# Attention over paged keys on one core: the read of the turned probabilities, one set of tables and one score change their places

## The chip, the cores and the metric

The kernel runs on one core of a Trainium2 chip. The metric is the device time of one execution in microseconds (us), as the median of several executions. The same kernel was also executed once under the hardware profiler; the views of the profile come from that one execution.

The core's engines each work through their own list of instructions, in order: PE (TensorE, the matrix multiplications, with PEld for the loads of its weights), DVE (VectorE), ACT (ScalarE), POOL (GpSimd) and SP (SyncE). An engine waits where its next instruction needs something that another engine or a transfer hasn't delivered, and all that stands behind it on the same engine waits too. Transfers between the core's memory and DRAM are issued by SP, ACT and POOL, each of which has a queue of its own, and are carried out by 16 DMA engines that all queues share.

## The reference

The input x has 8 sequences of 128 rows and 512 columns. Two layers follow, all in f32:

```python
x = x + L0_ffn(L0_cond(x, ...))        # weights picked by sequence; experts of rank 16
x = x + L1_ffn(L1_cond(x, ...))        # attention over a paged cache; 64 small experts
```

The change lies in the attention, L1_cond, which takes most of the time:

```python
q = x @ Wq.T ; k = x @ Wk.T ; v = x @ Wv.T      # 32 query heads, 8 key heads, 128 wide
q, k = rope(rmsnorm(q), pos), rope(rmsnorm(k), pos)
kc = k_cache[block_table] ; vc = v_cache[block_table]   # 16 pages of 32 keys for each sequence
scores = q @ [kc, k].T * SCALE                  # 512 cached keys and 128 new ones
scores = where(valid, scores, -1e30)
o = softmax(scores) @ [vc, v]
y = o @ Wo.T                                    # 4096 -> 512, summed over all heads
```

Four query heads share one key head.

## The kernel before

**Units and turns.** The attention is cut into 64 units. A unit is one sequence and one key head with its four query heads; two units that follow each other have the same sequence and the same half of the key heads, and share one set of gathered pages. Such a pair is called a step. The units are worked through in turns, and turn u holds work of several units at once: the scores and the softmax of unit u, the weighted sum of the values of unit u-2 (`values`), the output product of unit u-3 (`output`, `add_output`), and the projection and the norms of units that come later. The order on every engine is the one in which the code calls these helpers. That order is what the change edits.

**The products by fewer multiplications.** The projection and the output product work on pairs of sequences with 7 products in place of 8, so sums of inputs and weights are made beside them: `sums_x` and `sums_q` (their sum is recorded at line L163) for the projection, `sums_o` (L1031) for the output. Depending on u mod 4 and u mod 16 a turn holds different such work. The kinds u mod 4 = 0, 1, 2, 3 last differently for this reason; in turns with u mod 16 = 13, two of the sums of the projection's weights are done on DVE.

**A turn, in the order of the code** (`iteration`):

1. The pages of the *next* step. Turn u with u even gathers the first 8 of its 16 key pages, turn u odd the last 8: SP reads a page's number and issues a transfer of 32 KB (`gather`, L193) for each. Five are issued, then `exchange_in(u - 1)`, then the other three. So the keys of a step are complete when the last three pages of an odd turn have landed, and the first score of the following even turn needs them.
2. `exchange_in(u - 1)`: two reads on SP of what unit u-1 has written to DRAM, the turned queries and keys of unit u+1 (`qkb`, L933, 320 KB) and the turned probabilities of unit u-1 (`pT`, L936, 1280 KB, into one of two buffers that alternate).
3. `gather_v` (L203, POOL): two of the step's four groups of value pages, by an indirect transfer.
4. `make_tables` (L236, POOL): two products that hold the tables of the rotation for a step. It is called in turns 3, 5, 7, ... for the step of unit u+3; turn 3 makes those of step 3.
5. For each of the four query heads h: `scores(u, h)` on PE (L439: 128 x 512 against the pages; L442: 128 x 128 against the new keys), `mask_exp` (DVE L452 adds the mask and finds the lowest value, ACT L463 takes the exponential with its sum), `normalize` of the head before (DVE L468 the reciprocal, POOL L469 the product), at h = 2 `blocks_qk` (DVE L425: queries and keys of unit u+2, turned by blocks of 32 x 32, into the buffer `pb`), at h = 2 and 3 `blocks` (DVE L474: the probabilities turned by blocks, into `pb`), then `output(u - 3, h)` on PE (L1081) and, for h > 0, a product of the projection (PE L262, its sums on DVE L265).
6. `add_output(u - 3, ...)` (DVE L1150 and L1168: the sums of the output into `yp`), in an early and a late part; `heads_qk(u + 1)` (ACT L943: `qkb` into the order of the heads), `norms(u + 3)` (ACT L311 and L313, POOL L315 and L317).
7. The rest of `blocks`, then `exchange_out(u)` (L486): `pb` is written to DRAM as `px` in four transfers of 400 KB, two issued by SP and two by ACT.
8. `rotate(u + 3)` (DVE L329 to L347) and last on PE `values(u - 2)` (L956: ten passes of 512 columns that read `pT`).

**Who has how many buffers.** `pb` has one: `blocks_qk` of turn u writes it first, and so must wait until `px` of turn u-1 has been read out of it completely. `pT` has two, `px` in DRAM three. The banks into which PE writes scores are two, so a score needs the bank that `mask_exp` of the score before the last has read; the output product has one bank, `y`, and so its first product in a turn must wait for the `add_output` of the turn before.

**The full turn into DRAM and back.** What runs through one round: `blocks_qk` and `blocks` fill `pb`, `px` goes out, in the next turn `qkb` and `pT` come in; `qkb` is wanted at that turn's end by `heads_qk`, `pT` by `values` at the end of the turn after it. SP's queue holds, in this order and for each turn: five pages, `qkb`, `pT`, three pages, and SP's half of `px`.

Of the kernel before, what the change touches and what calls it, by code (L numbers as in the profile page):

```python
# [30 lines left out]
GH = 2  # L31
# [27 lines left out]
def adaln_ffn_kernel(  # L59
# [122 lines left out]
    def gather(step, first=0, end=NPP):  # L182
        hf, b = divmod(step, B)
        if first == 0:
            kv_t[step] = (
                kvp.tile([P, NPP, GH, PSIZE], F32, tag="kt", name=f"kt_{step}"),
                kvp.tile([P, LC, GH * D], F32, tag="vt", name=f"vt_{step}", bufs=3),
            )
        kt, vt = kv_t[step]
        for j in range(first, end):  # L190
            at = b * NPP + j
            page = nc.sync.value_load(pg[0:1, at : at + 1])
            nc.sync.dma_start(  # L193
                out=kt[:, j, :, :].rearrange("p g t -> p (g t)"),
                in_=kc[hf, ds(page, 1)].rearrange("o p f -> p (o f)"),
            )
# [237 lines left out]
    def scores(u, h, which=None):  # L434
        st, g = units[u]
        kt, _ = kv_t[st]
        qkT = qkT_t[u]
        s = banks(f"s_{u}_{h}", which)
        nc.tensor.matmul(  # L439
            out=s[:, :L], lhsT=qkT[:, h, :], rhs=kt[:, :, g % GH, :], start=True, stop=True  # L440
        )
        nc.tensor.matmul(  # L442
            out=s[:, L:NK], lhsT=qkT[:, h, :], rhs=qkT[:, REP, :], start=True, stop=True
        )
        s_t[u, h] = s

    def mask_exp(u, h):

        st, g = units[u]
        p = pp.tile([P, NK], F32, tag="p", name=f"p_{u}_{h}")  # L450
        low = stat.tile([P, 1], F32, tag="low", name=f"low_{u}_{h}")
        nc.vector.tensor_tensor_reduce(  # L452
            out=p,
            in0=s_t.pop((u, h))[:, :NK],
            in1=mask_t[st],
            scale=rs_t[u][:, h : h + 1],
            scalar=BIG,
            op0=ALU.add,
            op1=ALU.min,
            accum_out=low,  # L460
        )
        den = stat.tile([P, 1], F32, tag="den", name=f"den_{u}_{h}")
        nc.scalar.activation(p, p, AF.Exp, bias=low, scale=-1.0, accum_out=den)  # L463
        p_t[u, h], den_t[u, h] = p, den
# [460 lines left out]
    with ExitStack() as l1:  # L925
# [1 line left out]
        wk2 = l1.enter_context(tc.tile_pool(name="l1_2", bufs=2))  # L927

        def exchange_in(u):
            m = px_t.pop(u).rearrange("k b i f -> (k b) i f")  # L930
            if u + 2 in range(4, NU):
                qkb = wk1.tile([P, QD, NH * 32], F32, tag="qkb", name=f"qkb_{u + 2}")
                nc.sync.dma_start(out=qkb, in_=m[:, :, PW:])  # L933
                qkb_t[u + 2] = qkb
            pT = wk1.tile([P, QD, PW], F32, tag=f"pT{u % 2}", name=f"pT_{u}")
            nc.sync.dma_start(out=pT, in_=m[:, :, :PW])  # L936
            pT_t[u] = pT
# [325 lines left out]
        def iteration(u):  # L1263

            on = lambda v: 0 <= v < NU
            fb = LAST.get(u)
            r, group = u % 16, (u // 16 + 1) * GH
            f = room(fb) if fb is not None else None

            if u % 4 == 3:  # L1270
                k, j, four = (u + 5) // 4, 0, True
            elif u % 4 == 0:
                k, j, four = (u + 4) // 4, 0, False
            elif u % 4 == 1:
                k, j, four = (u + 3) // 4, 1, True
            else:
                k, j, four = (u + 2) // 4, 1, False
            slots = ()
            if 2 < u and k < NU // 4:
                slots = (1, 2, 6) if four else (4, 5, 3)  # L1280
            st = u // GH
            pages = on(u) and 1 < st + 1 < NQ * B
            first, end = ((0, 8), (8, NPP))[u % GH]
            if pages:
                gather(st + 1, first, first + 5)
            if on(u - 1):
                exchange_in(u - 1)
            if pages:
                gather(st + 1, first + 5, end)
            if pages:  # L1290
                gather_v(st + 1, u % GH * LC // GH, (u % GH + 1) * LC // GH)
            if on(u + 3) and u % GH == 1 and u > 1:
                make_tables(units[u + 3][0])
            if on(u - 3) and u % 4 == 3 and (u - 3) // 4 < WHOLE_PAIRS:
                load_y((u - 3) // 4)
            if u == 1:
                load_o(0, (0, B11), (2, B21))
            if NU - 5 <= u < NU - 1:
                load_whole(NQ * B - 4 + u - NU + 5)
            z_exchange(u - NU + 3)  # L1300
            if on(u - 3):
                evict_o(u - 3)
            if u >= NU and fb is not None:
                yT_t[fb] = f_turn(fb, *f)
            if u > NU:
                z = u - NU - 1
                z_turn(z, lambda n, shape: wo_t[:, slot(T4, NQ - 1), z * DM : (z + 1) * DM].rearrange("p (c s) -> p c s", c=NC))
            if u >= NU:
                z_blocks(u - NU + 4)
            if u in (2, 3):  # L1310
                norms(u + 3)
            for h in range(REP):
                if on(u):
                    if (u, h) not in ((1, 0), (1, 1), (2, 0)):
                        scores(u, h)
                        mask_exp(u, h)
                    if h > 0 and (u, h) != (1, 1):
                        normalize(u, h - 1)

                    if (u, h) == (1, 2):  # L1320
                        transpose_qk(3)

                    sums_o(u, h)
                    sums_w(u, h)
                    if 16 <= u < NU - 8 and (r, h) == (2, 3):
                        load_o(u // 16, (1, B12))

                    if h == 2:
                        new_pb(u)
                        if u + 2 in range(4, NU):  # L1330
                            blocks_qk(u + 2, u)
                    if h > 1:
                        blocks(u, h - 2)
                    if h == 1 and u == NU - 5:
                        f_fold()
                    if h == 3:
                        z_blocks(u - NU + 4)
                    if h == (1 if u == NU - 3 else 2) and fb is not None:
                        yT_t[fb] = f_turn(fb, *f)
                if on(u - 3):  # L1340
                    output(u - 3, h)
                    sums_a(u - 3, h)
                if h > 0 and slots:
                    project(k, j, slots[h - 1 : h])

                if (u, h) in WHOLE:
                    project_whole(1, *WHOLE[u, h])
            if on(u - 3):
                add_output(u - 3, False)
            if on(u + 1) and (u + 1) % GH == 0:  # L1350
                make_mask(units[u + 1][0])
            if u + 1 in range(4, NU):
                heads_qk(u + 1)

            if u < NU - 8:
                if r in LOADS_Q and u < NU - 16:
                    for n, i in LOADS_Q[r]:
                        load_q(group + n, i)
            if NU - 8 < u < NU - 2:
                f_weights(u - NU + 7)  # L1360
            if on(u):
                normalize(u, REP - 1)
            if 3 < u < NU - 3:
                norms(u + 3)
            if u == 1:
                scores(2, 0)
                mask_exp(2, 0)
            if on(u):
                blocks(u, REP - 2)
                blocks(u, REP - 1)  # L1370
                exchange_out(u)
            if on(u - 3):
                add_output(u - 3, True)
            if 16 <= u < NU - 8 and r in (0, 1, 2):
                n = u // 16
                load_o(n, *{0: ((0, B11),), 1: ((2, B21),), 2: ((3, slot(B22, n)),)}[r])
            if u == NU - 6:
                load_o(NQ - 1, (1, B12))
            if u + 3 < NU:
                rotate(u + 3)  # L1380
                if four and slots:
                    project(k, j, (7,))

            if u == NU - 6:
                rooms()

            ahead = u >= NU
            if ahead and on(u - 2):
                values(u - 2)
            if fb is not None:  # L1390
                f_gate(fb, *f_project(fb, yT_t.pop(fb), *f), *f)
            if not ahead and on(u - 2):
                values(u - 2)
# [164 lines left out]
```

## Time and profile before

| | before |
|---|---|
| runs | 1205.39, 1205.78, 1211.27 us |
| median of the runs | 1205.78 us |
| the profiled execution, its own time | 1209.55 us |
| span of its trace | 1207.8 us |
| mean granted clock of TensorE | 1.0 |
| DMA, mean over the span | 250 GB/s, 302.31 MB |
| SP's and ACT's queues, share of 16 engines | 53.2% in the one, 13.6% in the other |

The first layer ends at about 125 us; the turns take most of what follows. The lines below are the page's strip of 40 equal slices of the span, with each engine's busy share in tenths:

```profile
PE   9999999999999999999999999999999999999998
DVE  2647788787888787878887887879887888787632
POOL 3545769778755686578647685687657784643100
PEclk9999999999999999999999999999999999999999
DMA  8823777888888988888789978887989888898742
```

A digit 9 stands for 90% or more. PE is at 9 in every slice but the last, DVE and the DMA engines at 7 to 9 through the turns. The granted clock is full throughout.

The most costly groups on the other engines (line, engine, operation, out and in, count; then busy us, mean ns of one, idle us just before, and what ended most of it):

```profile
L463 ACT ACTIVATE p<-p,low 128x640 f32<-128x640 f32 x256 | 211.8, 828 | 433.7 <-DVE den L468 267.4
L469 POOL TENSOR_SCALAR p<-p,den 128x640 f32<-128x640 f32 x256 | 210.2, 822 | 233.4 <-DVE den L468 232.5
L452 DVE CUSTOM_DVE_ANT_0 p<-s,mask,rs 128x640 f32<-128x640 f32 x256 | 222.3, 878 | 81.6 <-PE s L442 80.7
L474 DVE STREAM_TRANSPOSE pb<-p 128x640 f32<-128x640 f32 x248 | 204.8, 826 | 25.6 <-POOL p L469 25.5
L203 POOL DMA_INDIRECT vt<-in_vc,vrow x128 | 137.6, 1075 | 40.8 <-issue 31.9
```

Idle time of ACT and POOL costs nothing by itself; it says only what they wait for.

### The profile page before, as it was taken

What the parts mean: (1) busy time and instruction counts of PE and PEld (TensorE: products, weight loads), DVE (VectorE), ACT (ScalarE), POOL (GpSimd) and SP (SyncE); (2) the same over time, 40 slices, a digit from 0 to 9 for tenths busy, and PEclk for the clock granted to TensorE, in tenths of its full rate; (3) what the DMA queues carried; (4) which work ended last, traced back from release to release, by engine and by line L of the source; (5) the groups of instructions that cost most, each with busy time, mean ns of one, the idle gap of its engine ahead of it and who ended that gap; (6) DMA issues with size and microseconds to landing.
All of it is one profiled execution on the core that took longest, in us unless ns stands there. A gap on an engine that the chain in (4) does not pass through costs nothing.

```text
span 1207.8 us, 16783 instructions
## 1 busy us (share of the span) xinstructions
PE 1194.7 (99%) x4156; PEld 714.6 (59%) x4156; DVE 913.1 (76%) x2103; ACT 504.3 (42%) x1457; POOL 740.4 (61%) x828
## 2 busy tenths in 40 slices
PE   9999999999999999999999999999999999999998
PEld 7666545565555556555556555555656555555554
DVE  2647788787888787878887887879887888787632
ACT  1345534443444444444444444444444444443211
POOL 3545769778755686578647685687657784643100
PEclk9999999999999999999999999999999999999999
DMA  8823777888888988888789978887989888898742
GB/s 315 287 89 113 247 238 245 263 265 264 264 253 257 301 244 278 260 287 282 237 258 282 294 240 281 285 289 246 279 255 302 254 263 251 261 281 230 232 140 97
DMA packets 205300, 302.31 MB, mean 250 GB/s; under 512 B 84755, under 2 KB 119316, under 8 KB 204180
## 3 DMA queue, kind: packets, MB, share of 16 engines
q1 hardware_dynamic: 170308, 196.81, 53.2%
q10 hardware_dynamic: 18576, 52.04, 13.6%
q0 software_dynamic: 16320, 52.40, 12.4%
q8 instruction: 33, 0.54, 0.2%
q14 instruction: 63, 0.52, 0.1%
HBM read 185.44 MB, written 115.74 MB: 249 GB/s over the span
## 4 chain that ended last, share of the span: by engine, by line
PE 82%; DMA 6%; POOL 4%; DVE 3%; issue 2%; SPq 1%; ACT 1%; ACTq 0%; DVEq 0%; POOLq 0%
PE o L956 18%; PE p L262 18%; PE s L439 16%; PE y L1081 13%; PE s L442 4%; PE p L295 3%; DMA px<-pb 2%; PE op L1445 2%; PE y L1094 2%; PE bp L648 1%; PE cp L626 1%; DMA kt<-in_kc 1%; PE fr L866 1%; POOL p L469 1%; DVE pb L474 1%
## 5 line engine op out<-in xcount | busy, mean ns | idle before, releaser
L463 ACT ACTIVATE p<-p,low 128x640 f32<-128x640 f32 x256 | 211.8, 828 | 433.7 <-DVE den L468 267.4
L469 POOL TENSOR_SCALAR p<-p,den 128x640 f32<-128x640 f32 x256 | 210.2, 822 | 233.4 <-DVE den L468 232.5
L452 DVE CUSTOM_DVE_ANT_0 p<-s,mask,rs 128x640 f32<-128x640 f32 x256 | 222.3, 878 | 81.6 <-PE s L442 80.7
L262 PE MATMUL p<-wqkv,xo 128*128 128x384 f32 x784 | 281.1, 487 | 0.7 <-DVE c L265 0.3
L439 PE MATMUL s<-kt,qkT 128*128 128x512 f32 x504 | 258.7, 595 | 4.5 <-DMA kt<-in_kc 2.6
L956 PE MATMUL o<-pT,vt 128*128 128x512 f32 x512 | 230.2, 592 | 0.0
L474 DVE STREAM_TRANSPOSE pb<-p 128x640 f32<-128x640 f32 x248 | 204.8, 826 | 25.6 <-POOL p L469 25.5
L1081 PE MATMUL y<-wo,oT 128*128 128x256 f32 x784 | 206.6, 380 | 0.9 <-DVE yp L1168 0.5
L262 PEld LDWEIGHTS p<-wqkv,xo 128*128 128x128 f32 x784 | 148.2, 190 | 70.2 <-POOL wqkv L163 1.6
L442 PEld LDWEIGHTS s<-qkT 128*128 128x128 f32 x504 | 95.8, 190 | 120.5 <-issue 120.5
L203 POOL DMA_INDIRECT vt<-in_vc,vrow x128 | 137.6, 1075 | 40.8 <-issue 31.9
L956 PEld LDWEIGHTS o<-pT,vt 128*128 128x128 f32 x512 | 97.2, 190 | 107.8 <-issue 92.8
L439 PEld LDWEIGHTS s<-kt,qkT 128*128 128x128 f32 x504 | 94.2, 190 | 78.3 <-issue 32.5
L1081 PEld LDWEIGHTS y<-wo,oT 128*128 128x128 f32 x784 | 131.9, 191 | 9.8 <-PE s L442 1.2
L311 ACT ACTIVATE sq<-c 128x128 f32<-128x128 f32 x320 | 98.8, 309 | 9.5 <-DVE oT L474 1.4
L442 PE MATMUL s<-qkT 128*128 128x128 f32 x504 | 96.8, 274 | 0.0
L317 POOL TENSOR_TENSOR rs<-ss,mhalf 128x5 f32<-128x5 f32 x64 | 82.2, 1284 | 5.3
L979 ACT COPY oT<-o 128x512 f32<-128x512 f32 x64 | 37.4, 585 | 102.3 <-PE o L956 77.2
L315 POOL TENSOR_SCALAR ss<-ss,eps 128x5 f32<-128x5 f32 x64 | 27.6, 431 | 74.3 <-ACT sq L311 74.3
L956 PE MATMUL o<-pT,vn 128*128 128x512 f32 x128 | 65.4, 592 | 0.0
L425 DVE STREAM_TRANSPOSE pb<-ca 128x640 f32<-128x640 f32 x60 | 50.2, 836 | 18.1 <-DMA px<-pb 8.2
L265 DVE TENSOR_TENSOR c<-c,p 128x384 f32<-128x384 f32 x84 | 44.9, 534 | 22.9 <-PE p L262 22.7
(198 smaller groups left out, 1441.3 us busy)
## 6 DMA issues: line engine op xcount, KB each, us to landing
pT<-px SPq DMA_DIRECT2D x64, 1280.0 KB, 6.6
px<-pb SPq DMA_DIRECT2D x120, 400.0 KB, 5.2
px<-pb ACTq DMA_DIRECT2D x120, 400.0 KB, 4.2
qkb<-px SPq DMA_DIRECT2D x60, 320.0 KB, 3.4
kt<-in_kc SPq DMA_DIRECT2D x512, 32.0 KB, 5.1
wqkv<-in_wqkv POOLq DMA_DIRECT2D x32, 384.0 KB, 4.8
wo<-in_wo POOLq DMA_DIRECT2D x17, 512.0 KB, 7.5
yd<-yp POOLq DMA_DIRECT2D x12, 512.0 KB, 9.0
```

The costliest lines, as they stand in the source:

```text
L203: nc.gpsimd.indirect_dma_start(out=kv_t[step][1][:, c, :], out_offset=None, in_=vc, in_offset=bass.IndirectOffsetOnAxis(ap=vrow[:, hf, at ...
L262: nc.tensor.matmul(out=ps, lhsT=xo[:, pr, x, c, :], rhs=w[:, c, :], start=(c == 0), stop=(c == 1))
L311: nc.scalar.activation(sq, cs[:, at : at + D], AF.Square, accum_out=ss[:, h : h + 1])
L317: nc.gpsimd.tensor_tensor(rs, ss, mhalf, ALU.pow)
L439: nc.tensor.matmul(out=s[:, :L], lhsT=qkT[:, h, :], rhs=kt[:, :, g % GH, :], start=True, stop=True)
L442: nc.tensor.matmul(out=s[:, L:NK], lhsT=qkT[:, h, :], rhs=qkT[:, REP, :], start=True, stop=True)
L452: nc.vector.tensor_tensor_reduce(out=p, in0=s_t.pop((u, h))[:, :NK], in1=mask_t[st], scale=rs_t[u][:, h : h + 1], scalar=BIG, op0=ALU.add, ...
L463: nc.scalar.activation(p, p, AF.Exp, bias=low, scale=-1.0, accum_out=den)
L469: nc.gpsimd.tensor_scalar(p_t[u, h], p_t[u, h], den, 1.0, ALU.mult, ALU.mult)
L474: nc.vector.transpose(pb_t[u][:, :, h * w : (h + 1) * w].rearrange("p i (j a) -> p j i a", a=32), p_t.pop((u, h)).rearrange("p (j i a) -> ...
L956: nc.tensor.matmul(out=o, lhsT=vt[:, c, j * D : (j + 1) * D] if c < LC else vn_t.pop(u), rhs=pT[:, c], start=(c == 0), stop=(c == LC),)
L1081: nc.tensor.matmul(out=y_t["y"][:, half * HN : (half + 1) * HN], lhsT=part(key)[:, i * S : (i + 1) * S], rhs=wo_t[:, slot(w, key[0] // (B ...
```

## The change

Three edits, each of which moves instructions and adds or removes none.

1. `exchange_in(u - 1)` keeps the read of `qkb` only. The read of `pT` becomes `probs_in(u - 1)`, called after the turn's last three pages. On SP's queue the order becomes five pages, `qkb`, three pages, `pT`, SP's half of `px`.
2. `make_tables(3)`, on POOL, is called in turn 2 behind the last `normalize`, no longer in turn 3 behind `gather_v`.
3. In the turns 5, 9, 13, ..., 61 the second score and its `mask_exp` are called ahead of the first head's output product, not behind it. On PE the order becomes score 0, score 1, output product 0, and then as before. DVE, ACT and POOL have the same order as before, since nothing of theirs stands between the two calls.

```diff
         def exchange_in(u):
-            m = px_t.pop(u).rearrange("k b i f -> (k b) i f")
+            m = px_t[u].rearrange("k b i f -> (k b) i f")
             if u + 2 in range(4, NU):
                 qkb = wk1.tile([P, QD, NH * 32], F32, tag="qkb", name=f"qkb_{u + 2}")
                 nc.sync.dma_start(out=qkb, in_=m[:, :, PW:])
                 qkb_t[u + 2] = qkb
+
+        def probs_in(u):
+            m = px_t.pop(u).rearrange("k b i f -> (k b) i f")
             pT = wk1.tile([P, QD, PW], F32, tag=f"pT{u % 2}", name=f"pT_{u}")
             nc.sync.dma_start(out=pT, in_=m[:, :, :PW])
             pT_t[u] = pT
...
                 exchange_in(u - 1)
             if pages:
                 gather(st + 1, first + 5, end)
+            if on(u - 1):
+                probs_in(u - 1)
             if pages:
                 gather_v(st + 1, u % GH * LC // GH, (u % GH + 1) * LC // GH)
-            if on(u + 3) and u % GH == 1 and u > 1:
+            if on(u + 3) and u % GH == 1 and u > 3:
                 make_tables(units[u + 3][0])
...
             for h in range(REP):
                 if on(u):
-                    if (u, h) not in ((1, 0), (1, 1), (2, 0)):
-                        scores(u, h)
-                        mask_exp(u, h)
+                    ahead = u > 1 and u % 4 == 1
+                    for n in (((0, 1), (), (2,), (3,)) if ahead else ((0,), (1,), (2,), (3,)))[h]:
+                        if (u, n) not in ((1, 0), (1, 1), (2, 0)):
+                            scores(u, n)
+                            mask_exp(u, n)
                     if h > 0 and (u, h) != (1, 1):
                         normalize(u, h - 1)
...
             if on(u):
                 normalize(u, REP - 1)
+            if u == 2:
+                make_tables(3)
             if 3 < u < NU - 3:
                 norms(u + 3)
```

`GH` is 2 (units in a step), `REP` is 4 (query heads of a unit), `NU` is 64.

## Prediction

> **What bounds the kernel now.** I read the page's busy shares first, then the costliest groups, the waits of TensorE, the timeline around them, and last the DMA issues.
>
> ```profile
> PE 1194.7 (99%) x4156; PEld 714.6 (59%) x4156; DVE 913.1 (76%) x2103; ACT 504.3 (42%) x1457; POOL 740.4 (61%) x828
> L439 PE MATMUL s<-kt,qkT 128*128 128x512 f32 x504 | 258.7, 595 | 4.5 <-DMA kt<-in_kc 2.6
> L1081 PE MATMUL y<-wo,oT 128*128 128x256 f32 x784 | 206.6, 380 | 0.9 <-DVE yp L1168 0.5
> L425 DVE STREAM_TRANSPOSE pb<-ca 128x640 f32<-128x640 f32 x60 | 50.2, 836 | 18.1 <-DMA px<-pb 8.2
> ```
>
> TensorE is busy all the time, so a change that removes no matmul can win only the small idle times; the third number behind the bar is all the idle ahead of the scores (4.5 us) and of the output products (0.9 us). The last line is the one place where VectorE stands waiting for a write of the turned probabilities (px).
>
> ```profile
> PE s L439 <- DMA kt<-in_kc: 2.6, 2, 1.6
> PE s L439 <- ACT oT L979: 0.7, 1, 0.7
> PE s L439 <- PE o L956: 0.6, 2, 0.4
> PE y L1081 <- DVE yp L1168: 0.5, 1, 0.5
> PE y L1081 <- DVE yp L1150: 0.4, 1, 0.4
> DVE pb L425 <- DMA px<-pb: 8.2, 11, 1.3
> ```
>
> The shown idle is too small. Eight passes of 512 columns last 3.60 us at 0.59 each, so they start (3.60-0.59)/7 = 0.43 apart, and a modelled end lies 0.16 behind the next possible start. I therefore count a stall from start to start:
>
> ```profile
> 567.94 0.38 PE L442 MATMUL s<-qkT 128*128 128x128 f32 x2
> 568.74 1.10 PE L1081 MATMUL y<-wo,oT 128*128 128x256 f32 x4 [0.41 <-DVE yp L1150]
> 577.27 0.54 SPq L933 DMA_DIRECT2D qkb<-px  x1
> 577.86 0.62 SPq L936 DMA_DIRECT2D pT<-px  x1
> 579.01 2.02 SPq L193 DMA_DIRECT2D kt<-in_kc  x3
> 584.26 1.02 PE L956 MATMUL o<-pT,vn 128*128 128x512 f32 x2
> 584.89 0.81 SPq L486 DMA_DIRECT2D px<-pb  x2
> 586.33 1.10 PE L439 MATMUL s<-kt,qkT 128*128 128x512 f32 x2 [1.04 <-DMA kt<-in_kc]
> 577.29 0.84 DVE L425 STREAM_TRANSPOSE pb<-ca 128x640 f32<-128x640 f32 x1 [0.69 <-DMA px<-pb]
> ```
>
> Turn 30's first score could start at 584.26 + 2 x 0.43 = 585.12 and starts at 586.33: 1.21 us lost. Its keys are the three pages issued from 579.01 on, behind the 1280 KB of pT. Done for every first score on new keys (even turns), the stalls are 1.76 (turn 4), 0.38 (14), 0.83 (18), 0.17 (24), 1.21 (30), 0.12 (34), 0.14 (52) and 0.59 (58): 5.2 us; in each the last page's packets end 0.7 to 1.25 us before the score starts, also where the waits view names ACT or PE. The pass behind each is some 0.08 late: 0.6. The output products of turns 13 and 29 lose 0.63 and 0.58 (568.74 against 567.94 + 0.22) and 0.15 on the passes behind them: 1.4. Sum: 7.2 us that the change can reach. All stalls of TensorE together are 17.9 us; 5.9 of these lie ahead of attention and the rest elsewhere.
>
> **The probabilities read behind the last three pages.** No instruction is added. The pages are issued 1.15 us sooner (at 577.86 instead of 579.01), and the transfer that stood ahead of them goes behind them.
>
> ```profile
> pT<-px SPq DMA_DIRECT2D x64, 1280.0 KB, 6.6
> px<-pb SPq DMA_DIRECT2D x120, 400.0 KB, 5.2
> px<-pb ACTq DMA_DIRECT2D x120, 400.0 KB, 4.2
> qkb<-px SPq DMA_DIRECT2D x60, 320.0 KB, 3.4
> kt<-in_kc SPq DMA_DIRECT2D x512, 32.0 KB, 5.1
> ```
>
> The gain of a page is bounded below by the sooner issue, 1.15, above by this plus the 3.55 us that pT's packets take of all 16 engines: 4.7. The lower end clears every stall but 0.06 in turn 30 and 0.6 in turn 4, the middle clears all; I take all, 5.8 with the passes behind, the low end being 5.1.
>
> Price: three page issues took 2.6 us from first to the one that would follow (10.83, 11.71 and 12.59 us after px's issue on the mean of turns 4 to 55), so pT is issued about 2.6 us later. Who waits for pT is values, a turn and more later; that is hidden, with some 10 us of cover. What stands behind pT on SP's queue is px of the same turn (584.89), which waits for VectorE anyway, so the issue isn't delayed. But pT's packets now end later than px's issue: before, the last one ends on the mean exactly at px's issue (from 3.0 before to 2.8 after). With 2.6 us more and the engines' share in those bins (0.55 to 0.8 busy today), 0.85 to 1.0 us of all engines' work is left when px is issued, against 0.09 today.
>
> What that does to px, the trace bounds from two sides. Turns 14 and 46 had 1.05 us of pT left, and px landed 9.24 and 8.93 us after its issue against 8.07 on the mean: 0.8 to 1.1 us later for each us left. Over all turns, though, px's landing grows only 0.08 us for each us that pT ends later. So px lands 0.1 to 1.0 later; I take 0.8, from the two turns that look like the changed ones.
>
> The Trainium skill (DMA: Bandwidth & Descriptors, section on queues, rings and completion order) has a rule that speaks against the edit: a DMA engine takes the descriptors of one issuer's ring in order and takes turns between rings by packet. By that SP's half of px stands behind all that is left of pT, and only ACT's half takes turns. Turns 14 and 46 agree with it, the slope over all turns doesn't; by the rule every turn's px would be later by all that is left, by the slope by nearly nothing.
>
> Who waits for px: the transpose of queries and keys (L425), which writes the single buffer pb that px is read from. It starts at the earliest 0.44 after px's last packet, and px's next issue comes 6.64 after it (mean; at least 6.4). The ring is 8.07 + 0.44 + 6.64 = 15.15 against an undisturbed mean turn of 16.15 (14.21, 17.23, 15.94, 17.23 for the four kinds): 1.0 us free. Queued behind the waiting L425 on VectorE are the transposes of the probabilities, the sums of the projection and mask_exp of the next score, for which TensorE's banks wait. In 18 turns L425 waits 0.5 us or more already; stalls of TensorE followed in 3, 13 and 29 alone. I therefore price 0.8 in an ordinary turn at nothing, covered by the 1.0, and at the full delay of about 1.0 where VectorE has no gap: turn 3, where px(2) and the pages collide today, and turns 13, 29 and 45, which have the 2.55 and 0.94 us of weight sums (L163) on VectorE. 4 turns x 1.0 = 4.0; bounds 0 (the slope) and +22 (the rival below). If the cover of 1.0 is gone, every turn pays what lies beyond it.
>
> **Turn 3's tables made in turn 2.** GpSimd's 0.83 + 0.97 us at 146.67 move ahead of turn 3's value pages (1.09 + 1.33). In turn 3 the sums of squares behind them (L315, 148.44) had their last input from ACT at 148.23, so at most 0.2 is won; the value pages come 1.8 later and are read some 50 us on. Bounds: 0.3 either way; taken as 0.
>
> **Second score ahead of the output in turns 5, 9, ..., 61.** On TensorE two passes of 0.43 and two of 0.11, 1.08 us, go ahead of the first output product, which therefore has 1.08 more for its wait on yp: this covers 0.63 and 0.58. The other engines keep their order. The output then comes 1.08 later, and its consumer add_output stands at the turn's end. Gain 0 to 1.4; taken as 1.4, since the products' wait is all there is. If VectorE is late beyond 1.08, the third score's bank waits instead.
>
> Sum: -5.8 - 1.4 + 0 + 4.0 = -3.2 us. On the profiled execution's own 1209.55 us (span 1207.8 and 1.75 around it) this is 1206.3; that execution is 3.8 above the median of the runs, 1205.78, and on the median it is 1202.6.
>
> **Rivals.**
> *Full gain.* The late px costs nothing, as the slope says, and 7.2 go: 1198.6. For it: no stall in 15 of the 18 turns in which L425 waits today. Against it: turns 14 and 46, and shares of the DMA engines near 1.0 in the six us after px's issue, where a delay isn't made good.
>
> *The px ring takes over (slower).* Place: L425's wait for px in every turn; it decides once px lands more than 1.0 later on the mean. A later px makes the reads of the next turn later, so pT's rest grows with the delay. At a ring of 15.15 + delay, pT would end 12.3 + 6.6 - 15.15 = 3.7 us past px's issue rather than 2.6; the added 1.1 at a share of 0.8 makes 1.85 us left, times 0.8 a delay of 1.4 to 1.5, so 0.4 a turn more than the free 1.0. Over 56 turns +22, less 7: 1221. With 0.3 a turn, 1215. For it: L425 is the only wait of VectorE for px, and 18 turns are at its edge. Against it: a mean of 0.85 left is below the point.
>
> *It does nothing that shows.* The first score waits for something else at the same moment (rotated queries through ACT, or the banks), and the stall stays: 1205.8. Against it: qkb lands 1.35 us or more ahead of its use, and the pages' packets end last at all eight stalls.
>
> **How the numbers follow.** Forecast 0.45, its own range 1199.8 to 1206.5 (costs between 1.2 and 8); full gain 0.27; the ring 0.20; nothing 0.08. A measurement of this kernel tells 0.5%, 6.0 us, from no change. Faster than 1199.75 are most of the full gain (0.23) and the edge of the forecast (0.04): 0.27. Slower than 1211.8 is the ring without its mild end (0.17) and a forecast with turns 3, 13, 29 and 45 mis-sized (0.02): 0.19. The rest, 0.54, is within. The range runs from just below the full gain, 1197.5, to a mild ring, 1213; half of the ring's chance lies above it.
>
> **What would show it.** Right: no idle ahead of L439 from kt, pages' packets ending 2 us or more before each even turn; pT's packets ending 2 to 3 us past px's issue; px landing near 8.9; L425's wait grown from 8.2 us to 20 or more without a longer undisturbed turn; no idle ahead of L1081 from yp. Wrong: turns 36 to 39 longer than 14.21, 17.23, 15.94 and 17.23 (the ring), px landing at 8.1 (full gain), or first scores that still start late with their pages long there.

## The result, and the profile after

The changed kernel takes 1219.24 us in the median of 6 runs (1217.17 to 1223.87), the kernel before, run beside it, 1206.33. The ratio is 1.0108, with a 95% interval from 1.008 to 1.0137: 13 us slower, where 3 us less had been forecast.

The profiled execution took 1223.87 us, with a span of 1222.0. Of its 14.2 us over the span before, 2.9 are there by the end of turn 2: in the first 20 us the granted clock of TensorE was 0.83 in this execution and 1.0 in the one before, and at 38 us, ahead of anything that the change touches, TensorE is already 2.9 us behind. The other 11.3 us come in turns 3 to 60.

The costliest groups of the changed kernel's page (line, engine, operation, out and in, count; busy us, mean ns, idle us ahead and what ended most of it):

```profile
L262 PE MATMUL p<-wqkv,xo 128*128 128x384 f32 x784 | 282.3, 488 | 8.1 <-POOL wqkv L163 4.4
L425 DVE STREAM_TRANSPOSE pb<-ca 128x640 f32<-128x640 f32 x60 | 50.4, 840 | 62.3 <-DMA px<-pb 45.0
```

L425 stood idle for 18.1 us before and for 62.3 now; the projection's idle time grew from 0.7 to 8.1. TensorE's waits in the changed kernel (us in total, times, longest):

```profile
PE p L262 <- POOL wqkv L163: 4.4, 6, 1.2
PE p L262 <- DVE c L265: 3.8, 4, 2.7
PE s L439 <- DVE low L452: 3.8, 4, 1.6
...
PE y L1084 <- DVE yp L1153: 1.9, 2, 1.4
```

No wait for key pages is left: that part of the change did what it says. In its place stand waits for DVE and for GpSimd's weight sums, none of which was longer than 0.5 us before. GpSimd itself stands idle ahead of none of these sums (L163): it comes to them late, though the loads of the weights land later as well (6.7 us after their issue, 4.8 before). On the chain of work that ended last, which the page follows back from the last instruction, px's transfers have 11% of the span; before they had 2%. Last the page's DMA issues, with the median us to landing:

```profile
px<-pb SPq DMA_DIRECT2D x120, 400.0 KB, 6.3
px<-pb ACTq DMA_DIRECT2D x120, 400.0 KB, 8.0
...
kt<-in_kc SPq DMA_DIRECT2D x512, 32.0 KB, 3.0
```

A page lands 3.0 us after its issue instead of 5.1. The medians of px's writes, 5.2 and 4.2 before, can't be compared with these: of ACT's 120 writes the trace before tells the landing of 2 alone, the trace after that of 62. So I go by the packets. In turns 4 to 59, pT's rest at px's issue is 1.75 us of all engines' time (0.09 before), SP's half of px ends 7.48 us after its issue (6.52), ACT's half, the one that counts, 8.63 (8.05).

**Turn by turn.** I measured each turn from one end of `values` to the next and took its excess over the shortest that the same turn has in any profiled execution of this study. Before, the excess is 6.8 us in even turns, where new keys are first used, and 3.6 in odd ones; after, 2.9 and 18.8. The even turns 4, 14, 18, 24, 30, 34 and 58 won 5.6 us. Most other turns are the same to 0.01 us. The loss sits in few: against before, turn 3 is 1.9 us longer, 5 0.9, 9 0.6, 11 0.5, 13 1.3, 25 0.5, 27 0.7, 29 2.3, 37 0.4, 41 2.8, 43 2.3, 45 0.8, 52 0.5 and 60 1.4.

Turn 41 shows how. SP's issues, then DVE and TensorE, from the timelines of the changed kernel:

```profile
765.86 2.02 SPq L193 DMA_DIRECT2D kt<-in_kc  x3
767.97 0.61 SPq L939 DMA_DIRECT2D pT<-px  x1
772.37 0.81 SPq L486 DMA_DIRECT2D px<-pb  x2
...
771.50 0.84 DVE L474 STREAM_TRANSPOSE pb<-p 128x640 f32<-128x640 f32 x1 [1.30 <-POOL p L469]
...
773.60 1.97 PE L1084 MATMUL y<-wo,oT 128*128 128x256 f32 x8 [1.35 <-DVE yp L1153]
...
782.18 0.84 DVE L425 STREAM_TRANSPOSE pb<-ca 128x640 f32<-128x640 f32 x1 [2.86 <-DMA px<-pb]
...
784.24 1.56 PE L262 MATMUL p<-wqkv,xo 128*128 128x384 f32 x4 [0.54 <-DVE c L265]
```

The turn loses in two places. At its start the output product waits for the sums of turn 40 (yp). They stand on DVE behind the last transposes of the probabilities, which wait for GpSimd, and this lateness goes back to L425 of turn 40, which had stood 2.63 us for px. Then the same again: pT goes out 4.4 us ahead of px and so is still under way when px starts. px's last packet lands late, L425 stands for 2.86 us (0.82 in this turn before), and TensorE's projection, whose bank the sums behind L425 have to empty, waits in turn. Counted from start to start, the two places cost 1.5 and 0.7 of the turn's 2.8 us.

What the pages ahead of pT do to the engines is seen in windows of 2 us that end at px's issue in turn 40 (763.00 before, 772.37 after). Before, then after; the last two columns are the DMA engines' busy share and GB/s:

```profile
757.00:759.00 2.00, 2.00 (x10) 1.42 (x9) 2.00 (x7) 0.15 (x1) 0.07 (x1) 1.00 1.01 316
759.00:761.00 2.00, 2.00 (x6) 0.89 (x5) 1.82 (x4) 1.97 (x7) 2.00 (x3) 1.00 1.03 406
761.00:763.00 2.00, 2.00 (x6) 0.95 (x5) 0.88 (x2) 1.63 (x9) 1.46 (x4) 1.00 1.04 318
```

```profile
766.37:768.37 2.00, 2.00 (x6) 0.95 (x5) 2.00 (x7) 0.14 (x1) 0.07 (x1) 1.00 0.68 188
768.37:770.37 2.00, 2.00 (x6) 0.69 (x5) 1.83 (x4) 1.97 (x7) 2.00 (x3) 1.00 0.55 97
770.37:772.37 2.00, 1.88 (x8) 0.97 (x6) 0.87 (x2) 1.64 (x9) 1.47 (x4) 1.00 0.97 366
```

Before, the engines were full in these six us. Now they are 0.68, 0.55 and 0.97 busy, since SP spends some 2.6 us on three issues of 32 KB while 1280 KB wait behind them on its queue. On the mean of turns 8 to 55 the six bins of one us ahead of px's issue hold 5.3 us of engine time before and 4.1 after: 1.2 us a turn are left unused, and this work runs against px instead.

### The profile page after: what moved, and what is told of

It reads as the page before. It is cut to its first block, busy times and chain, and to the rows that moved or that the text cites. A ratio compares the mean times of both kernels' runs of the same rounds, so it can differ in the third digit from the quotient of the medians.

```text
span 1222.0 us, 16843 instructions
## 1 busy us (share of the span) xinstructions
PE 1199.0 (98%) x4156; PEld 715.8 (59%) x4156; DVE 910.6 (75%) x2103; ACT 502.0 (41%) x1457; POOL 740.1 (61%) x828
## 4 chain that ended last, share of the span: by engine, by line
PE 64%; DMA 12%; POOL 10%; DVE 6%; issue 4%; ACT 2%; SPq 1%; ACTq 1%; DVEq 0%; POOLq 0%
PE o L959 14%; PE p L262 12%; PE s L439 11%; DMA px<-pb 11%; PE y L1084 8%; POOL p L469 3%; PE s L442 3%; DVE pb L474 3%; PE p L295 3%; PE bp L648 2%; PE op L1454 2%; PE cp L626 2%; PE y L1097 2%; POOL wqkv L163 2%; ACT sq L311 1%
## 5 line engine op out<-in xcount | busy, mean ns | idle before, releaser
L425 DVE STREAM_TRANSPOSE pb<-ca 128x640 f32<-128x640 f32 x60 | 50.4, 840 | 62.3 <-DMA px<-pb 45.0
L317 POOL TENSOR_TENSOR rs<-ss,mhalf 128x5 f32<-128x5 f32 x64 | 84.9, 1326 | 5.3
L315 POOL TENSOR_SCALAR ss<-ss,eps 128x5 f32<-128x5 f32 x64 | 24.6, 384 | 78.0 <-ACT sq L311 77.8
L1153 DVE TENSOR_TENSOR yp<-yp,y 128x512 f32<-128x512 f32 (+3 forms) x94 | 60.1, 639 | 0.0
```

The source lines that it names most:

```text
L317: nc.gpsimd.tensor_tensor(rs, ss, mhalf, ALU.pow)
```

## The experiments

Theory 1 was the px ring: the late pT makes px late, and L425 carries that to TensorE. Theory 2 was the second score: eight of the turns that lost most have u mod 4 = 1, which are just the turns of the third edit. The table sums up what each execution left; "left" is pT's rest at px's issue in us of all engines' time, "lands" is px's last packet after its issue, "L425" its idle time in all, and the last two are the excess of odd and even turns.

| run | median us | ratio to before (95%) | left | lands | L425 | odd | even |
|---|---|---|---|---|---|---|---|
| before | 1206.33 | | 0.09 | 8.08 | 18.1 | 3.6 | 6.8 |
| changed | 1219.24 | 1.0108 (1.0080 to 1.0137) | 1.75 | 8.65 | 62.3 | 18.8 | 2.9 |
| e1 | 1217.60 | 1.0088 (1.0062 to 1.0114) | 1.68 | 8.47 | 53.7 | 17.8 | 1.8 |
| e2 | 1205.89 | 1.0007 (0.9984 to 1.0029) | 0.08 | 8.00 | 15.6 | 1.5 | 4.9 |
| e3 | 1207.02 | 1.0000 (0.9982 to 1.0019) | 0.07 | 7.93 | 17.6 | 3.7 | 5.9 |
| e4 | 1208.11 | 1.0010 (0.9991 to 1.0028) | 0.69 | 8.30 | 37.7 | 5.6 | 1.4 |
| e5 | 1216.77 | 1.0082 (1.0058 to 1.0106) | 1.14 | 8.41 | 41.3 | 8.5 | 8.9 |
| e6 | 1215.49 | 1.0054 (1.0033 to 1.0075) | 0.15 | 8.36 | 44.4 | 9.9 | 5.4 |
| e7 | 1309.42 | 1.0820 (1.0792 to 1.0848) | 1.86 | 10.49 | 144.5 | 102.2 | 7.3 |
| e8 | 1283.10 | 1.0630 (1.0596 to 1.0664) | 0.02 | 9.90 | 131.2 | 64.3 | 14.5 |
| e9 | 1202.67 | 0.9967 (0.9954 to 0.9980) | 0.03 | 7.96 | 19.4 | 4.2 | 0.7 |
| e10 | 1201.82 | 0.9978 (0.9967 to 0.9988) | 0.00 | 7.78 | 10.4 | 2.9 | 0.2 |

**One part at a time.** e1 is the first edit alone:

```diff
+            if on(u - 1):
+                probs_in(u - 1)
             if pages:
                 gather_v(st + 1, u % GH * LC // GH, (u % GH + 1) * LC // GH)
```

> Only the read of the turned probabilities (pT) goes behind the last three key pages; tables and scores as before. Theory 1 (px's ring): pT's rest stands ahead of px, px lands 0.5 to 0.6 us later than 8.07 on the mean, VectorE's L425 waits for it, and this edit alone gives the loss: page stalls -5.8, late turns about +17, so +9 to +13 us (ratio 1.008 to 1.011), L425's waits for px 40 us or more. Theory 2 (the second score ahead delays the output and what follows it on PE, DVE and POOL): this edit alone wins its page stalls, -4 to -6 us (ratio 0.995 to 0.997).

e2 is the third edit alone, e3 the second and third without the first:

> Only the second score ahead of the first output product in turns 5, 9, ..., 61. Theory 1: -1.4 to 0 us (ratio 0.999 to 1.000), the output's two waits of turns 13 and 29 gone, the other turns with u mod 4 = 1 at 17.23 us as before. Theory 2: the turns 5, 9, 13, 25, 29, 37, 41 and 45 grow as in the changed kernel, +8 to +13 us (ratio 1.007 to 1.011).

> All of the change but the move of pT: tables of step 3 made in turn 2, second score ahead. Theory 1: within 2 us of before (ratio 0.998 to 1.001); turn 3, 17.45 us from the end of turn 2 to its own end before and 19.34 in the changed kernel, stays at 17.0 to 17.6. Theory 2: +8 to +13 us. If the tables in turn 2 are what made turn 3 longer, turn 3 is at 19 us here too.

e1 has the loss, e2 and e3 have none: theory 2 is out, and the loss belongs to the move of pT. The second score ahead brought turns 13 and 29 down to 17.23 and 17.31 us in e2, as expected, but that is under what the timed runs can tell; and in e3, which has the same edit, turn 29 kept 18.19 us, since the projection waited 0.60 us for GpSimd's weight sums there. Turn 3 was 17.8 us in e2 and 18.0 in e3, so the moved tables do nothing here. Beside the late pT it was 20.8 without them (e1) and 19.3 with them; with one execution each that stays open. e2 and e3 also show how far single traces agree: they differ only in the tables, and their turns 3 to 60 by 3.2 us in all.

e4 and e5 have pT late in odd or in even turns only:

```diff
+            late = u % GH == 1        # e5: u % GH == 0
+            if on(u - 1) and not late:
+                probs_in(u - 1)
             if pages:
                 gather(st + 1, first + 5, end)
+            if on(u - 1) and late:
+                probs_in(u - 1)
```

> pT behind the last three pages only in odd turns, where those pages complete the keys of the next turn; in even turns pT stays ahead of them. Theory 1: all page stalls gone (-5.8), px late only in odd turns; a turn that follows makes part of it good, so the loss is under half of 17: between -3 and +3 us (ratio 0.9975 to 1.0025). Theory 2: -4 to -6 us, as with the move in every turn.

> pT behind the last three pages only in even turns, whose pages nobody awaits before the turn after next: the cost by itself, with no page stall removed. If the cost comes with each late pT wherever it stands, about half of the 15 to 17 us that the move in every turn costs: +5 to +9 us (ratio 1.004 to 1.0075). If it needs two late turns one after the other (the ring feeding on itself), and single ones are made good by the next turn's free 1.0 us, -1 to +2 us (ratio 0.999 to 1.002).

e4 removes the page stalls (even excess 1.4). In the trace its turns 3 to 60 are 3.4 us shorter, which is no more than e2 and e3 differ by, and the timed runs show no gain, so its cost is about as large as its gain. e5 wins nothing in even turns (excess 8.9) and is 9.5 us slower, a little over the 5 to 9 that were expected. A single late pT costs by itself; no two in a row are needed.

**Order on the queue, or engine time?** e7 lets ACT issue all of px, so that none of it stands behind pT in SP's ring; e8 is the control with pT early.

```diff
-            eng = nc.sync if i < QD // 2 else nc.scalar
+            eng = nc.scalar
```

> pT late in every turn, as in the run of that edit alone, and all four transfers of px issued by ACT, none by SP, so that no part of px stands behind pT in SP's ring. If px is late because its SP half waits in order behind pT's rest, it lands at about the time that the next run (the same issue by ACT with pT early) shows, and the time is within 3 us of that run's. If it is the 16 engines' time that pT's rest and px share, px lands 0.4 to 0.6 us later than in that run, and the time is 7 to 12 us above it.

> The control: the kernel before with all four transfers of px issued by ACT. Both theories: the time of before within some us (ACT issues twice as many, 0.85 us more a turn, and is 42% busy), px landing between 7.8 and 9.0.

px lands 0.59 us later in e7 than in e8, as much as with both queues (0.57). So the delay needs no place behind pT in SP's ring: it is the engines' time that pT's rest takes from px. The two hardly run side by side. In e7 px's first packet starts 2.54 us after the issue (1.01 in e8), when pT's last is about to end (2.69), and 3% of px's packets start before that end; of ACT's half in the changed kernel it is 5%. Why px on another queue lets pT's rest go first, the traces don't show. In time e7 is 26 us above e8, where 7 to 12 were expected; TensorE's granted clock was 0.983 in e7's profiled execution and 0.992 in e8's, and it was busy for 1226.1 us and 1217.6, so some of the 26 us is a slower TensorE.

My expectation for e8 was far off, and that taught more: px takes 6.45 us of engine time instead of 5.6 and lands 1.8 us later, and the kernel takes 76 us more.

```profile
DVE pb L425 <- DMA px<-pb: 131.2, 53, 5.0
```

That is e8's wait view: L425 now waits in 53 turns, where it did for px in 11 before. But px's landing isn't all that changed. ACT issues the last of the four transfers 3.2 us after the first (0.5 with two issuers), and is held meanwhile: its copy of the outputs (L979) has 266 us of idle time ahead of it, 102 before. And TensorE, at a granted clock of 0.992, is busy for 1217.6 us instead of 1194.7. How the 76 us divide among the later px, the held ACT and the slower TensorE was not tested, so no price per us of landing can be read from e8. In the changed kernel 0.57 us more of landing went with about 17 us paid (11.3 net and the 5.6 won).

e9 and e10 change the amount: only a quarter of the probabilities is read, late in e9 and early in e10.

```diff
-            pT = wk1.tile([P, QD, PW], F32, tag=f"pT{u % 2}", name=f"pT_{u}")
-            nc.sync.dma_start(out=pT, in_=m[:, :, :PW])
+            pT = wk1.tile([P, 1, PW], F32, tag=f"pT{u % 2}", name=f"pT_{u}")
+            nc.sync.dma_start(out=pT, in_=m[:, :1, :PW])
```

> The move of pT in every turn as in the run of that edit alone, but only a quarter of the turned probabilities (320 of 1280 KB) is read, and values uses this quarter four times; TensorE's work is unchanged. If the cost comes from pT's rest that shares the engines with px, it goes with the amount: pT left at px's issue under 0.4 us, px landing no later than in the next run, and the time within 2 us of it. If it comes from the order on SP (pT's issue behind the pages, SP held up), the cost of 15 to 17 us stays, and this run lies 10 us or more above the next.

> The control: the kernel before, with the same quarter of pT read in its old place ahead of the last pages. Both theories: 0 to 8 us faster than before, since the pages stand behind a transfer of a quarter of the size and px lands 0.3 us or more sooner.

Both leave three quarters of the probabilities out. They lie 0.9 us apart, with the same order on SP as in e1 and before, whose distance is 11 us. The order costs nothing that the timed runs tell when the transfer is small (px lands 0.18 us later in e9 than in e10). Theory 1 holds, with its mechanism: pT's work that is left when px starts.

**Tries at a version that beats both.** e6 leaves pT and shifts pages to the even turn:

```diff
-            first, end = ((0, 8), (8, NPP))[u % GH]
+            first, end = ((0, 11), (11, NPP))[u % GH]
```

> Nothing of the change. pT stays where it was; of a step's 16 key pages the even turn gathers 11 (5 ahead of qkb and pT, 6 behind) and the odd turn 5, all ahead of qkb. So the keys are complete without pT going behind anything. If the page stalls were caused by pT ahead of the last pages, they go here too, and px is not late: -4 to -6 us (ratio 0.995 to 0.997), px landing at 8.0 to 8.2. If six pages behind pT hold up SP until px is due, px is issued late in even turns and L425 waits more: +2 to +8 us.

The page stalls go, but SP's half of px is late in even turns; SP's timeline in e6, turn 28:

```profile
562.83 4.53 SPq L193 DMA_DIRECT2D kt<-in_kc  x6
568.31 5.40 SPq L486 DMA_DIRECT2D px<-pb  x2
```

The two issues of px, 0.81 us in other turns, stretch over 5.40 behind six pages. In e11 and e12 ACT issues an odd turn's last three pages, behind the second exponential or at the turn's start; both have the second score ahead.

```diff
+                    if h == 1 and by_act:          # e12: ahead of evict_o
+                        gather(st + 1, first + 5, end, nc.scalar)
```

> A version meant to beat both: pT stays where it was; the last three pages of an odd turn are issued by ACT behind the second exponential, so that they stand behind nothing of pT in SP's ring; second score ahead as in the change. If the page stalls come from the order in SP's ring, they go and px isn't late: 7 us less, less what ACT's three issues (some 0.9 us each) delay the later exponentials: -7 to -2 us (ratio 0.994 to 0.998). If the pages are late because of the engines' share that pT takes, or if ACT is late with its exponentials, 0 to +6 us.

> The same, with ACT issuing the three pages at the start of the odd turn, ahead of its copy of the output transposes (L979). The pages then share the engines with px (3 x 0.14 us), not with pT: page stalls gone, px 0.2 to 0.4 us later in every second turn: -6 to +1 us (ratio 0.995 to 1.001).

e11 took 1207.12 us (ratio 1.0017, 1.0003 to 1.0030), e12 1216.92 (1.0092, 1.0071 to 1.0114). In neither does TensorE wait for pages. In e12 ACT's copy of the outputs stands behind the page issues; its waits put down to transfers are 160 us in all, and turn 3 alone is 6.9 us longer than before; at 11 us more than before it missed its expectation. In e11 the trace's excess falls to 8.3 us, from 10.4 before, which is less than single traces differ by, and the timed runs show no gain; it lies in the range that was given for late pages or a late ACT. No wait for pages shows, and ACT's part was not tested.

e13 to e15 ask which work behind L425 carries the delay: the projection's sums of the third head go ahead of L425 on DVE.

```diff
-                    if h == 2:
-                        new_pb(u)
-                        if u + 2 in range(4, NU):
-                            blocks_qk(u + 2, u)
...
                 if h > 0 and slots:
                     project(k, j, slots[h - 1 : h])
+                if on(u) and h == 2:
+                    new_pb(u)
+                    if u + 2 in range(4, NU):
+                        blocks_qk(u + 2, u)
+                    blocks(u, 0)
```

> The changed kernel, with L425 and the first block transpose moved on DVE behind the projection's sums of the third head (0.5 to 1.0 us of L265, whose matmuls are done by then). If the lateness reaches TensorE through the projection's banks, TensorE's waits for DVE c L265 (3.8 us in the changed kernel) go and each late turn wins 0.5 us or more: 6 to 12 us less than the changed kernel (ratio to before 0.999 to 1.004). If it goes through the mask pass and normalize to GpSimd, whose places do not move, 0 to 3 us less (ratio 1.006 to 1.011).

> The kernel before with the second score ahead and the same order on DVE; pT in its old place. L425 waits rarely here, so under both readings little changes: -3 to +1 us (ratio 0.9975 to 1.001); page stalls stay.

> pT behind the pages in odd turns only, second score ahead, sums ahead of L425: the run with pT late in odd turns was 1.2 us above before. If the projection's banks were the route, its cost of some 5 us falls to 2 or less and it beats before: -5 to -1 us (ratio 0.996 to 0.999). If not, -1 to +2 us.

e13 took 1222.68 us (1.0128, 1.0097 to 1.0160), e14 1216.02 (1.0084, 1.0053 to 1.0115), e15 1211.83 (1.0034, 1.0017 to 1.0052). In e13 TensorE's waits for the projection's sums are gone, and it is no faster: its waits for the mask pass are 6.7 us (3.8 in the changed kernel) and those for GpSimd's weight sums 4.5 (4.4). So the projection's banks are one route among several, and closing it wins nothing. e14 went against my expectation. DVE now waits 73.5 us for TensorE's projection, 57.7 of them directly ahead of L425, so L425 starts 1.3 to 2.6 us after px's last packet (means of the four kinds of turn) instead of 0.9 to 1.3; its wait for px falls to 0.4 us, and the kernel is 9 us slower, with an excess of 6.6 us in odd turns and 11.0 in even ones, where first scores wait for pages again. A late L425 is thus paid like a late px: the likely reading, not shown by itself, is that the round of L425, px, reads and pages has little room, wherever the time is put in. e15, with hardly a wait for px left at L425 (1.1 us idle in all), is 4 us slower than before and missed both of its ranges. No version that computes the same beat the kernel before. A second buffer for pb, which would take L425 out of the round and so test it directly, wasn't tried; it would take 12.8 KB of each partition.

## Why the prediction was wrong, step by step

- *The page stalls.* Right: 5.8 us forecast, 5.6 gone in the trace's even turns. For the timed runs the sum was too rich: e10, in which the page stalls are gone too and px lands sooner, wins 2.7 us by its ratio (1 - 0.9978 of 1206). The stalls were read from an execution 3.8 us above the median. That a usual one has far fewer isn't borne out: e2 and e3, with the pages in the old order, have an excess of 4.9 and 5.9 us in even turns, though partly in other turns (36 and 48). Why the timed runs pay less for them stays open.
- *The second score* took 0.9 and 0.7 us off turns 13 and 29 in e2, as worked out, but none off turn 29 in e3; and in the changed kernel the late px puts 2.2 and 3.2 us of excess into the same turns, and the output products still wait for yp (2.5 us in all, 0.9 before).
- *The tables* at nothing: e2 and e3 agree.
- *What is left of pT.* pT's last packet ends 2.6 us past px's issue, as forecast (2.6), but that is 1.75 us of work, not 0.85 to 1.0. I turned lateness into work with the shares of before. The failed step there: the two us in which pT now isn't issued yet had been full (0.99, 0.98) and are now half empty (0.45, 0.43).
- *px's landing.* 0.8 us later was forecast, 0.57 measured. The slope was 0.3 for each us left, well under the 0.8 that I took from two turns. One reason is in the bins: in the first us behind px's issue the engines were 0.53 busy before and are 1.02 now, so part of pT's rest fills time that stood empty.
- *The term that failed*: "4 turns x 1.0 = 4.0", with the delay of an ordinary turn priced at nothing, "covered by the 1.0". The trace shows some 17 us paid (11.3 net, and the 5.6 that were won), in 14 turns, with 0.4 to 2.8 each. The room was also too rich: the 6.64 us from L425 to the next px are what the shortest stretch of each kind of turn gives on the mean (6.38 and three times 6.73), while in the turns where L425 waited 0.5 us or more they are 6.9 in both kernels, which leaves 0.7 of the 1.0. The mean delay is still below that, but px's landing spreads (0.95 us standard deviation after, 0.73 before), and in turns 9 to 13, 25 to 30 and 40 to 43 L425 awaits a px that landed 8.4 to 10.5 us after its issue. In or beside these stretches GpSimd loads and sums the next weights as well. A late landing alone doesn't decide: turns 51 and 59, with 10.3 and 10.2, lost 0.2 us and nothing.
- *The cover*, measured instead of assumed: in the changed kernel and e1, waits of L425 below 2 us left all 17 turns with u mod 4 = 3 at 17.2 to 17.3 us; waits above 2.5 us lengthened all 10 odd turns that had one, between turns 6 and 57. In turns with u mod 4 = 1 no such limit shows: in the changed kernel turns 5, 37 and 45, with waits of 0.9 to 1.4 us, are 0.4 to 1.0 above their shortest. An even turn lets its own wait pass (3.65 us in turn 28 at no cost) and the next odd turn pays (turn 29, 20.4 us). Before, no wait was above 1.3.
- *The rule on rings*, which spoke against the edit: the Trainium skill (DMA: Bandwidth & Descriptors, queues, rings and completion order) lets SP's half wait for pT's rest in its ring. The trace agrees for that half, 0.96 us later; but ACT's half, behind nothing of pT, ends last in both kernels and is 0.58 later, and e7 against e8 shows the same delay without the ring. What the rule says of taking turns between rings shows little here: ACT's half has its first packet 2.48 us after its issue (1.79 before), when pT's last one is about to end (2.57). So it is pT's rest on the shared engines that decides, and not which ring px stands in.
- *The rival that came true in its sum* is the px ring, with 1221 forecast for it. Its place was right and so was its amount left (1.85, measured 1.75). Its condition was not, that px lands more than 1.0 us later on the mean (0.57), nor its delay of 1.4 to 1.5, nor its distribution: it had 0.4 us in each of 56 turns, and undisturbed turns kept 14.21, 17.23, 15.94 and 17.23 us (of turns 36 to 39, the sign that was named, 37 is 0.4 longer and the others at most 0.07). That its sum lies near the measured 1219.24 is luck. I gave it 0.20 because a mean delay stayed below a mean room.

## What to carry to other kernels

A transfer that moves behind small ones doesn't just come later: while the issuer works through the small ones, the DMA engines may stand half idle, as here, and that time is missing where the next large transfer starts. Look at the engines' share in the very us that the move opens. Compare a delay with the room turn by turn, with the spread of both, not mean against mean: here the mean delay was below the mean room, and the turns with the longest waits and those behind them paid. And a round through one buffer (write, wait, refill) can be lengthened by what is put into it on any of its engines. Try such edits one by one: here three were one loss and two nothings.

## What the runs showed of the hardware that was not expected

- The same 1600 KB in the same four transfers landed 8.1 us after the first issue through two issuers' queues and 9.9 through one (e8), with 5.6 and 6.45 us of all engines' time. With one issuer the last issue came 3.2 us after the first instead of 0.5; counted from the last issue, one queue landed sooner (6.7 us against 7.6).
- An issuer can be held by its own transfers: in e8 ACT's four issues stretch over 4.4 us (median), where its two took 0.85 before, and its copy of the outputs waits behind them.
- px on ACT's queue hardly starts before pT's rest on SP's queue has ended (3% of its packets in e7).
- In the changed kernel px's own packets took less engine time (4.9 us instead of 5.6), for a reason that the trace doesn't show; 1.75 us of pT's rest delayed px by 0.57 only.
